# Moving a group norm to ScalarE and block sums to accumulating transfers in a two-attention convolution kernel

## The chip, the cores and the metric

The kernel runs on one core of a Trainium2 chip. Its engines work side by side: TensorE (PE, with its weight loads as PEld) multiplies, VectorE (DVE) and ScalarE (ACT) do elementwise work, GpSimd (POOL) a little of it, and SyncE (SP) only starts transfers. [...] The metric is the device time of one execution in microseconds (us).

## The reference

Sixteen images of 256 channels and 32 x 32 = 1024 positions pass through two blocks in float32. The source is cut to what is computed:

```python
def attention_block(x, w_proj, b_proj, w_out, b_out):     # 4 heads of 64
    xs = x.reshape(B, C, H * W).transpose(0, 2, 1)
    q, k, v = split(xs @ w_proj + b_proj)
    o = softmax(q @ k.T / sqrt(64)) @ v
    return (o @ w_out + b_out + xs).transpose(0, 2, 1).reshape(B, C, H, W)

def second_block(x):
    x = x + attention(group_norm(x, gn1_w, gn1_b))        # 8 heads of 32
    h = conv1x1(group_norm(x, gn2_w, gn2_b), mlp_w1, mlp_b1)   # 256 -> 1024
    return x + conv1x1(gelu(h), mlp_w2, mlp_b2)                # 1024 -> 256
```

A group norm takes 32 groups of 8 channels; its mean and variance run over 8 x 1024 values.

## The kernel before

**Tiling.** An image is held as 128 partitions x 2 channel halves x 1024 positions (`x`, three of them in rotation). Positions are cut into two halves t of 512 (`TB`), so that a product of 128 x 512 fills one bank of PSUM, the memory that TensorE writes. [...] three double tiles `s0`, `s1`, `s2` that `wide` hands out, the one longest unused first unless a number is given or a tile is kept back (`kept`), and two single banks `b0`, `b1` that `bank` hands out. A tile that is handed out again must first have been read by its last user.

**Stages of an image.** `attention_a` is the first attention: for 32 units it makes scores (`s_a`, L390), exponentials on ScalarE (`e_a`, L398), weighted values two units later (`acc_a`, L411) and sums of exponentials on VectorE (`es_a`, L423). When a half of the queries is done, the denominators are made (`den_a`, L442), copied by ScalarE, sent by a transfer to be spread over partitions, inverted on VectorE (L359), sent back through DRAM as `d_a`, and multiplied in (L468). The projection (`o`, L336) adds the result to `x` (L663) and takes the statistics of norm g (L666). In odd items of this attention the double tile `s2` holds the accumulator, and two double tiles are left for the scores.

Norm g of the image is worked out in the *gap* between the first attention and the keys and queries of the second (`qk_b`), and the gap is filled with *hidden pieces*: the first matrix of the MLP of the image before. `attention_b` is the second attention (`s_b` L524, `e_b` L539, `es_b` L555, `acc_b` L576, `den_b` L598), and its fill is the second matrix of the MLP of the image before (*output pieces*) and the first attention's keys, queries and values of the image after. The last projection of `attention_b` and norm h of the image are handed on into `attention_a` of the next image: norm h is applied there, among the exponentials, for images 0 to 14. While an attention runs, products are cut into narrow ones (`cols[0]` is 64 or 32 there); in the gap and for the last image's norm h, `cols[0]` is 128, which is `P`.

**The norm.** `group_norm` is a chain of steps with waits between: `averages` multiplies by a matrix that averages over groups (`gm`, `gv`), GpSimd takes the power -1/2 (L734), VectorE makes the scale and shift (`ga`, `gc`, L736 to L740), and L746 applies them: four VectorE operations of 128x512. For norm h five sums and differences of the result follow (`sums_of_input`, L875 to L879).

**The MLP** is made of two products in the manner of Strassen and Winograd, each with seven block products in place of eight. `begin`, `middle` and `finish` treat one of four row blocks each (i = 0 to 3), in the order begin 0, 1, middle 0, 1, finish 0, 1, and the same for 2, 3. Their products are L898, their evictions L911, L923 to L925 and L938, L939. Each `finish` ends with two subtractions (`combine` with minus, L954) between the four results of the Gelu. `reduce` makes a product of the second matrix; its order is 2, 5, 3, 4, 1, 6, 7. For products 2, 3, 4 the result is copied out of PSUM into `lent` by ScalarE and added to two blocks of `x` by VectorE (L1013), and then `combine` with plus adds four blocks for a later product (L954). When a block of `x` has all its sums, SP sends it out.

**Order.** The program's order is written out by hand: pieces are called in the order above, and `Later` calls a step after a number of ticks (a tick follows each unit and each piece). A scheduler then places instructions on their engines; `keep_in_program_order` pins one among its neighbours.

Of the kernel before, what the change touches and what calls it, by code (L numbers as in the profile page):

```python
# [8 lines left out]
F32 = mybir.dt.float32  # L9
I32 = mybir.dt.int32  # L10
AF = mybir.ActivationFunctionType
ALU = mybir.AluOpType
AX = mybir.AxisListType

P = 128
# [223 lines left out]
def first_pass(ctx, tc, x, out, k):  # L239
    nc = tc.nc  # L240
    B, C, S = x.shape
# [6 lines left out]
    small = ctx.enter_context(tc.tile_pool(name="small", bufs=2))  # L248
# [36 lines left out]
    def use(n):  # L285
        order.remove(n)
        order.append(n)

    def wide(name, n=None):
        if n is None:  # L290
            n = next(m for m in order if m not in kept)
        use(n)
        return ps_s.tile([P, 2, TB], F32, tag=f"s{n}", name=name)

    def bank(name, n):
        return ps_a.tile([P, TB], F32, tag=f"b{n}", name=name)
# [34 lines left out]
    cols = [P]  # L331
# [358 lines left out]
    def group_norm(key, src, stats, gw, gb, tag, out_tile, wait, then=None):  # L690
        st = {}

        def averages(name, src):
            if cols[0] == P:
                ps = bank(name, 1)
                product(ps[:, :CC], k["gavg"], src, start=True, stop=True)
                return [(slice(0, P), ps[:, :CC])]
            ps = wide(name)  # L700
            halves = [slice(h, h + HALF) for h in range(0, P, HALF)]
            for n, sl in enumerate(halves):
                nc.tensor.matmul(
                    ps[sl, n, :CC], k["gavg"][sl, sl], src[sl], start=True, stop=True
                )
            return [(sl, ps[sl, n, :CC]) for n, sl in enumerate(halves)]

        def means():
            mv = small.tile([P, CC, 2], F32, tag="mv", name=f"mv_{key}")
            for cc in range(CC):  # L710
                nc.vector.bn_aggr(mv[:, cc, :], stats[:, cc].rearrange("p t k -> p (t k)"))
            mean_c = small.tile([P, CC], F32, tag="mean_c", name=f"mean_c_{key}")
            nc.vector.tensor_copy(mean_c, mv[:, :, 0])
            st.update(mv=mv, mean_c=mean_c)
            later.after(wait, variances)

        def variances():
            mean = small.tile([P, CC], F32, tag="mean", name=f"mean_{key}")
            for sl, ps in averages(f"gm_{key}", st["mean_c"]):
                nc.vector.tensor_copy(mean[sl], ps)  # L720

            dv = small.tile([P, CC], F32, tag="dv", name=f"dv_{key}")
            nc.vector.tensor_sub(dv, st["mean_c"], mean)
            nc.vector.tensor_mul(dv, dv, dv)
            tv = small.tile([P, CC], F32, tag="tv", name=f"tv_{key}")
            nc.vector.tensor_add(tv, dv, st["mv"][:, :, 1])
            st.update(mean=mean, tv=tv)
            later.after(1 if cols[0] == P else 2, apply)

        def apply():  # L730
            rstd = small.tile([P, CC], F32, tag="rstd", name=f"rstd_{key}")
            for sl, ps in averages(f"gv_{key}", st["tv"]):
                nc.vector.tensor_scalar(rstd[sl], ps, EPS, None, ALU.add)
            nc.gpsimd.tensor_tensor(rstd, rstd, k["mhalf"], ALU.pow)  # L734
            a = small.tile([P, CC], F32, tag="ga", name=f"ga_{key}")
            nc.vector.tensor_mul(a, rstd, gw)  # L736
            ma = small.tile([P, CC], F32, tag="gma", name=f"gma_{key}")
            nc.vector.tensor_mul(ma, st["mean"], a)
            c = small.tile([P, CC], F32, tag="gc", name=f"gc_{key}")
            nc.vector.tensor_sub(c, gb, ma)  # L740
            y = act.tile([P, CC, S], F32, tag=tag, name=f"gn_{key}")
            out_tile.append(y)
            for t in range(NT):
                sl = slice(t * TB, (t + 1) * TB)
                for cc in range(CC):
                    nc.vector.tensor_scalar(  # L746
                        y[:, cc, sl], src[:, cc, sl],
                        a[:, cc : cc + 1], c[:, cc : cc + 1], ALU.mult, ALU.add,
                    )
            if then:  # L750
                then(y)

        means()
# [133 lines left out]
    def mlp(b, xb):  # L887
        n4 = HC // 2
        gs, open_sums = {}, {}
# [23 lines left out]
            )  # L913

        def begin(i):
            ps = wide(f"m1_{b}_{i}")
            if i % 2 == 0:
                open_sums["once"] = wide(f"m1_{b}_{i}_1")
            once = open_sums["once"][:, i % 2, :]
            open_sums[i] = ps  # L920
            products_of(i, [(2, ps[:, 0, :], True), (5, ps[:, 1, :], True), (1, once, True)])
            minus, rest = unit(0, 1, i), unit(1, 1, i)
            nc.scalar.activation(minus, ps[:, 0, :], AF.Copy, scale=-1.0)  # L923
            nc.vector.tensor_sub(rest, minus, ps[:, 1, :])  # L924
            nc.vector.tensor_add(rest, rest, once)  # L925
# [8 lines left out]
        def finish(i):  # L934
            ps = open_sums.pop(i)
            products_of(i, [(7, ps[:, 0, :], False), (6, ps[:, 1, :], False)])
            rest = gs[1, 1, i]
            nc.vector.tensor_add(unit(0, 0, i), rest, ps[:, 0, :])  # L938
            nc.vector.tensor_add(rest, rest, ps[:, 1, :])  # L939
            gelu(0, 0, i, gs[0, 0, i])  # L940
            gelu(1, 1, i, rest)
            combine((1, 0), (0, 0), False, i)
            combine((0, 1), (1, 1), False, i)

        hidden = [
            lambda part=part, i=i: part(i)
# [3 lines left out]

        def combine(to, what, plus, only=None):
            for i in range(n4) if only is None else (only,):
                d = gs[(*to, i)]
                (nc.vector.tensor_add if plus else nc.vector.tensor_sub)(  # L954
                    d, d, gs[(*what, i)]
                )

# [14 lines left out]
        def reduce(number, right, outs, then):  # L974
            ps = wide(f"m2_{b}_{number}")[:, 0, :]
            for i in range(n4):
                product(
                    ps, blocks[2][number - 1][:, i * P : (i + 1) * P], gs[(*right, i)],
                    start=(i == 0), stop=(i == n4 - 1),
                )  # L980
            bias, num = None, 1
            if len(outs) == 1:
                bias = k["m2b2"]

                num = 2 if b == B - 1 and number == 7 else 1
            elif number in (2, 5):
                bias = k["m2b"]
            co = outs[0][0]
            if len(outs) == 2:

                if not lent:
                    lent.append(act.tile([P, 4, TB], F32, tag="v0", name=f"lent_{b}"))
                m = lent[0][:, number % 4]
                if bias is not None:
                    nc.scalar.activation(m, ps, AF.Identity, bias=bias[:, co : co + 1])
                    bias = None
                else:
                    nc.scalar.copy(m, ps)
                ps = m

            def add_up():
                for co, t, plus in outs:
                    missing[co, t] -= 1
                    n = TB // num
                    for u in range(num):
                        sl = slice(t * TB + u * n, t * TB + (u + 1) * n)
                        y, p = xb[:, co, sl], ps[:, u * n : (u + 1) * n]
                        if bias is not None:
                            nc.vector.scalar_tensor_tensor(
                                y, p, bias[:, co : co + 1], y, ALU.add, ALU.add  # L1010
                            )
                        else:
                            (nc.vector.tensor_add if plus else nc.vector.tensor_sub)(y, y, p)  # L1013
                        if not missing[co, t]:
                            nc.sync.dma_start(out[b, co * P : (co + 1) * P, sl], y)
                if then:
                    combine(*then, True)


            if len(outs) == 2 and b < B - 1:  # L1020
                later.after(1, add_up)
            else:
                add_up()
# [32 lines left out]
    ps, n = bank("bqk", 0), brow.shape[0]  # L1056
# [32 lines left out]
    for b in range(B):  # L1089
# [3 lines left out]
        if b:  # L1093
# [4 lines left out]
                lambda st, b=b, xn=xn: group_norm(  # L1098
                    f"g{b}", xs[b], st, k["g1w"], k["g1b"], "res", xn, 2 if b else 3
                ),  # L1100
# [13 lines left out]
        n = len(qk) // CC  # L1114
# [352 lines left out]
```

## Time and profile before

| | us |
|---|---|
| median of 3 runs | 3700.3 (3698.66 to 3700.75) |
| profiled execution | 3700.6 |
| its span in the trace | 3698.8 |
| period of an image | 228.6 (one image of 230.3) |
| L746 norm h, 64 operations of 128x512 on VectorE | 30.6 |
| L746 norm g, 64 operations of 128x512 on VectorE | 30.6 |
| L1013, 160 operations on VectorE | 102.9 |
| GpSimd's transfers, all queues' bytes | 6.2 of 138.4 MB |

Busy times are sums over instructions of one engine within the span; engines work side by side, so they don't add up to the span. A group of instructions is written as line, engine, operation, output, inputs and shapes, with the count, the busy time and the mean of one. A timeline's row has the start and the time of a run of like instructions, and in square brackets how long the engine had been idle before it and what it waited for. The mean of one operation in a group is longer than the distance between two in a row, since neighbours overlap: the four operations of norm h take 1.92 us together at a mean of 543 ns.

### The profile page before, as it was taken

The numbers are of one execution on the slowest core, as the hardware profiler recorded it, in microseconds if no ns is written. First come the engines' busy times: TensorE is split into PE (matmuls) and PEld (weight loads), VectorE is DVE, ScalarE is ACT, GpSimd is POOL, SyncE is SP. The second block draws the span as 40 slices with busy tenths as digits, with TensorE's granted clock in tenths as the row PEclk, the third lists the DMA queues.
The fourth block names the chain that finished last, engine by engine and source line by source line (L and its number), as shares of the span: only waits on it lengthen the run. The fifth ranks groups of instructions, "written<-read, shape, count | busy, mean of one in ns | idle before, by whom it ended". The sixth has DMA issues, their size and how long they took to land.

```text
span 3698.8 us, 79399 instructions
## 1 busy us (share of the span) xinstructions
PE 3644.9 (99%) x34221; PEld 1290.8 (35%) x34221; DVE 2688.2 (73%) x3486; ACT 2118.4 (57%) x2768; POOL 121.1 (3%) x266
## 2 busy tenths in 40 slices
PE   9999999999999999999999999999999999999999
PEld 4333333333333333333333333333333333333333
DVE  4686767767677776777777777787777877677777
ACT  4665646556565665646656465564655656556572
POOL 3000000000000000000000000000000000000000
PEclk9999999999999999999999999999999999999999
DMA  4000110101101011010110101001010010101100
GB/s 146 11 16 30 53 33 13 50 30 53 33 14 50 30 53 33 19 49 28 50 33 19 50 27 50 32 19 50 27 56 27 23 46 33 50 27 42 36 28 27
DMA packets 66548, 138.35 MB, mean 37 GB/s; under 512 B 35630, under 2 KB 36398, under 8 KB 61966
## 3 DMA queue, kind: packets, MB, share of 16 engines
q1 hardware_dynamic: 63116, 126.64, 10.7%
q8 instruction: 270, 4.42, 0.5%
q0 software_dynamic: 1328, 6.17, 0.5%
q14 instruction: 88, 0.72, 0.1%
q10 hardware_dynamic: 1746, 0.40, 0.1%
HBM read 111.17 MB, written 21.23 MB: 36 GB/s over the span
## 4 chain that ended last, share of the span: by engine, by line
PE 81%; DVE 14%; issue 3%; DMA 1%; ACT 1%; POOL 1%; SPq 0%; DVEq 0%; ACTq 0%
PE s_b L524 12%; PE acc_b L576 12%; PE m L336 10%; PE s_a L390 9%; PE acc_a L411 8%; PE m L898 6%; PE qk_a L336 6%; PE qk_b L336 5%; DVE es_a L423 4%; PE v_a L336 3%; PE j L336 3%; PE v_b L336 2%; PE den_b L598 1%; DVE g L954 1%; DVE es_b L555 1%
## 5 line engine op out<-in xcount | busy, mean ns | idle before, releaser
L539 ACT ACTIVATE e_b<-s_b 128x1024 f32<-128x1024 f32 (+1 forms) x1280 | 983.0, 864 | 151.0 <-PE s_b L524 151.0
L555 DVE TENSOR_TENSOR es_b<-es_b,e_b 128x1024 f32<-128x1024 f32 x768 | 899.1, 1218 | 217.3 <-ACT e_b L539 217.2
L398 ACT ACTIVATE e_a<-s_a 128x1024 f32<-128x1024 f32 x512 | 521.3, 1025 | 360.1 <-PE s_a L390 345.7
L524 PE MATMUL s_b<-q,k 32*64 32x512 f32 x8192 | 526.9, 601 | 9.8 <-DVE v L793 7.0
L390 PE MATMUL s_a<-q,k 64*64 64x512 f32 x4096 | 532.6, 593 | 1.1
L411 PE MATMUL acc_a<-e_a,v 64*64 64x512 f32 x4096 | 528.5, 589 | 0.0
L423 DVE TENSOR_TENSOR es_a<-es_a,e_a 128x1024 f32<-128x1024 f32 x384 | 471.0, 1226 | 58.4 <-ACT e_a L398 39.1
L576 PE MATMUL acc_b<-e_b,v 128*32 128x512 f32 x4096 | 493.8, 600 | 0.0
L336 PE MATMUL m<-g,w 128*32 128x512 f32 (+1 forms) x3320 | 404.3, 592 | 0.0
L524 PEld LDWEIGHTS s_b<-q,k 32*64 32x64 f32 x8192 | 166.1, 130 | 337.3 <-issue 127.7
L411 PEld LDWEIGHTS acc_a<-e_a,v 64*64 64x64 f32 x4096 | 161.9, 133 | 277.5 <-issue 236.1
L390 PEld LDWEIGHTS s_a<-q,k 64*64 64x64 f32 x4096 | 152.6, 133 | 278.1 <-issue 208.2
L898 PE MATMUL m<-gn_h,w 128*128 128x512 f32 x512 | 243.7, 604 | 5.7 <-DVE g L924 3.3
L589 DVE TENSOR_TENSOR res_b<-res_b,acc_b 128x512 f32<-128x512 f32 x192 | 131.6, 686 | 145.5 <-PE acc_b L576 145.5
L336 PE MATMUL qk_b<-gn_g,wq 128*32 128x512 f32 (+1 forms) x1280 | 235.7, 594 | 1.7
L576 PEld LDWEIGHTS acc_b<-e_b,v 128*32 128x32 f32 x4096 | 108.6, 109 | 358.2 <-ACT e_b L539 194.8
L336 PE MATMUL qk_a<-x,wp 128*32 128x512 f32 (+1 forms) x1856 | 233.5, 592 | 0.0
L336 PEld LDWEIGHTS m<-g,w 128*32 128x32 f32 (+1 forms) x3320 | 121.4, 112 | 262.3 <-issue 235.0
L954 DVE TENSOR_TENSOR g<-g,g 128x512 f32<-128x512 f32 x320 | 206.0, 680 | 4.0 <-ACT g L911 2.8
L898 PE MATMUL m<-hs,w 128*128 128x512 f32 x384 | 177.9, 592 | 0.1
L555 DVE TENSOR_TENSOR es_b<-e_b,e_b 128x1024 f32<-128x1024 f32 x128 | 150.6, 1217 | 0.0
L911 ACT ACTIVATE g<-g,m1b 128x512 f32<-128x512 f32 x128 | 92.1, 722 | 99.6 <-DVE g L938 72.7
(146 smaller groups left out, 2793.5 us busy)
## 6 DMA issues: line engine op xcount, KB each, us to landing
w<-w_kept SPq DMA_DIRECT2D x30, 1792.0 KB
d_a<-row_a SPq DMA_DIRECT2D x64, 256.0 KB
rd_b<-row_b SPq DMA_DIRECT2D x252, 64.0 KB
out_dram<-x SPq DMA_DIRECT2D x63, 256.0 KB
x<-in_x_dram SPq DMA_DIRECT2D x30, 512.0 KB
w_kept<-w_made POOLq DMA_DIRECT2D x2, 1792.0 KB, 7.1
w_made<-in_L_conv_mlp_w_dram POOLq DMA_DIRECT2D x8, 256.0 KB, 6.5
x<-in_x_dram SPq DMA_DIRECT2D x4, 256.0 KB
```

Source lines behind the costliest of these rows:

```text
L336: nc.tensor.matmul(o[sl], w[:, sl], r, **flags)
L390: nc.tensor.matmul(s[h : h + HALF, g, :], kT[g * D : (g + 1) * D, c, kb * P + h : kb * P + h + HALF], qT[g * D : (g + 1) * D, c, t * TB : ...
L398: nc.scalar.activation(e, s, AF.Exp, scale=float(D) ** -0.5)
L411: nc.tensor.matmul(accs[i][h][g * D : (g + 1) * D, :], v[h * HALF : (h + 1) * HALF, kb, c * 2 + g], e[h * HALF : (h + 1) * HALF, g, :], st ...
L423: nc.vector.tensor_add(sums[i], held[i] if kb == 1 else sums[i], e)
L524: nc.tensor.matmul(outs[g][h : h + HALF, :], kT[g * D : (g + 1) * D, c, k0 : k0 + HALF], qT[g * D : (g + 1) * D, c, t * TB : (t + 1) * TB] ...
L539: nc.scalar.activation(to, s, AF.Exp, scale=float(D) ** -0.5)
L555: ins = nc.vector.tensor_add(d, es[n % 2] if kb == 0 else d, es[n])
L576: nc.tensor.matmul(acc[g * D : (g + 1) * D, :], v[:, kb + m, c * G + g], es[2 * m + g // 2][:, g % 2, :], start=(m == 0), stop=(m == 1),)
L589: nc.vector.tensor_add(r, r, acc)
L898: nc.tensor.matmul(ps, blocks[1][number - 1][:, i * P : (i + 1) * P], inputs[b][number], start=first, stop=True, skip_group_check=not first,)
L954: (nc.vector.tensor_add if plus else nc.vector.tensor_sub)(d, d, gs[(*what, i)])
```

## The change

- *Norm h on ScalarE.* Where `cols[0]` isn't `P` (norm h of images 0 to 14) the four operations of a norm become ScalarE activations with the scale and shift as per-partition operands. Norm g and the last norm h stay on VectorE.
- *The averages in the gap* go into the double tile `s2` and no longer into the bank `b1`.
- *The hidden pieces' PSUM.* `begin(i)` takes the double tile i % 2 and the bank i % 2; before, it took double tiles in turn, and two row blocks shared one more of them.
- *An early Gelu* of 128x1 in `begin(0)`.
- *The subtractions* of the four row blocks come after `finish(3)`, all eight of them, pinned in order; for the last image they stay where they were.
- *Sums by transfers.* For images 0 to 14 the additions of `combine` with plus and of `reduce` for products with two outputs, where they are plain sums, become transfers that GpSimd starts and that add to what stands at their destination. Subtractions and the additions with a bias stay on VectorE.

```diff
@@ group_norm, averages
             if cols[0] == P:
-                ps = bank(name, 1)
+                ps = wide(name, 2)[:, 0, :]
@@ group_norm, apply
-                    nc.vector.tensor_scalar(
-                        y[:, cc, sl], src[:, cc, sl],
-                        a[:, cc : cc + 1], c[:, cc : cc + 1], ALU.mult, ALU.add,
-                    )
+                    if cols[0] == P:
+                        nc.vector.tensor_scalar(
+                            y[:, cc, sl], src[:, cc, sl],
+                            a[:, cc : cc + 1], c[:, cc : cc + 1], ALU.mult, ALU.add,
+                        )
+                    else:
+                        nc.scalar.activation(
+                            y[:, cc, sl], src[:, cc, sl], AF.Identity,
+                            bias=c[:, cc : cc + 1], scale=a[:, cc : cc + 1],
+                        )
@@ mlp, begin
-            ps = wide(f"m1_{b}_{i}")
-            if i % 2 == 0:
-                open_sums["once"] = wide(f"m1_{b}_{i}_1")
-            once = open_sums["once"][:, i % 2, :]
+            if i == 0:
+                few = small.tile([P, 1], F32, tag="few", name=f"few_{b}")
+                tc.keep_in_program_order(
+                    nc.scalar.activation(few, k["mhalf"][:, :1], AF.Gelu)
+                )
+            ps, once = wide(f"m1_{b}_{i}", i % 2), bank(f"m1_{b}_{i}_1", i % 2)
@@ mlp, finish
-            combine((1, 0), (0, 0), False, i)
-            combine((0, 1), (1, 1), False, i)
+            for n in (i,) if b == B - 1 else range(n4) if i == n4 - 1 else ():
+                combine((1, 0), (0, 0), False, n)
+                combine((0, 1), (1, 1), False, n)
@@ mlp, combine
-                d = gs[(*to, i)]
-                (nc.vector.tensor_add if plus else nc.vector.tensor_sub)(
-                    d, d, gs[(*what, i)]
-                )
+                d, g = gs[(*to, i)], gs[(*what, i)]
+                if plus and b < B - 1:
+                    nc.gpsimd.dma_start(d, g, accum_op=ALU.add)
+                    continue
+                ins = (nc.vector.tensor_add if plus else nc.vector.tensor_sub)(d, d, g)
+                if not plus:
+                    tc.keep_in_program_order(ins)
@@ mlp, reduce, add_up
+                        elif plus and b < B - 1:
+                            nc.gpsimd.dma_start(y, p, accum_op=ALU.add)
                         else:
                             (nc.vector.tensor_add if plus else nc.vector.tensor_sub)(y, y, p)
```

## The prediction

> **What bounds the kernel now.** I read the page's busy times first, then TensorE's waits, then windows over one image, then the timeline of the stretches that the change touches.
>
> ```profile
> PE 3644.9 (99%) x34221; PEld 1290.8 (35%) x34221; DVE 2688.2 (73%) x3486; ACT 2118.4 (57%) x2768; POOL 121.1 (3%) x266
> ```
>
> TensorE is the bound, at a granted clock of 1.00: 3698.8 - 3644.9 = 53.9 us of the span is all that work elsewhere can win. What does TensorE wait for?
>
> ```profile
> PE den_a L442 <- DVE res_a L428: 28.1, 15, 1.9
> PE s_b L524 <- DVE v L793: 7.0, 16, 1.2
> PE m L898 <- DVE g L924: 3.3, 15, 1.0
> ```
>
> Total, times, longest. One wait stands out: 28.1 / 15 = 1.87 us per image, and VectorE ends it. Windows over a typical image (start 674.9, period 228.6 us) are two parts of the first attention, the gap (hidden pieces and norm g), the queries and keys, and the second attention; the columns are wall time, then busy time of PE, PEld, DVE, ACT and POOL.
>
> ```profile
> 674.90:710.40 35.50, 35.50 (x340) 12.37 (x344) 21.50 (x21) 21.37 (x23) 1.69 (x4) 1.00 0.21 69
> 710.40:738.80 28.40, 26.50 (x248) 9.41 (x248) 26.08 (x42) 14.38 (x15) 0.70 (x1) 1.00 0.07 20
> 738.80:770.30 31.50, 31.19 (x101) 13.39 (x101) 21.51 (x44) 12.98 (x20) 1.14 (x3) 1.00 0.06 18
> 770.30:805.00 34.70, 34.37 (x364) 13.53 (x368) 21.36 (x24) 23.21 (x32) 0.00 (x0) 1.00 0.15 54
> 805.00:903.30 98.30, 98.30 (x1140) 30.62 (x1132) 77.02 (x89) 60.49 (x84) 2.00 (x6) 1.00 0.09 28
> ```
>
> Only the second row loses much (1.90 us), and there VectorE is full (26.08 of 28.40). In the second attention TensorE loses nothing, although VectorE is busy for 77.02 us.
>
> [...] The trace's nearest rows are lower: a Gelu of that shape from SBUF with one pointer, 722 ns, and an Identity from PSUM, 688 ns. The trace decides. [...] the trace has copies between exponentials without a load. [...] The eight 256 KB loads on that queue landed in 3.5 to 10.4 us here, median 7.1[...].
>
> **Part A: ScalarE normalises norm h, in the first attention.**
>
> ```profile
> 718.45 1.02 ACT L398 ACTIVATE e_a<-s_a 128x1024 f32<-128x1024 f32 x1 [0.69 <-PE s_a L390]
> 720.28 1.02 ACT L398 ACTIVATE e_a<-s_a 128x1024 f32<-128x1024 f32 x1 [0.81 <-PE s_a L390]
> 722.30 0.16 DVE L740 TENSOR_TENSOR gc_h<-g2b,gma_h 128x2 f32<-128x2 f32 x1
> 722.49 1.92 DVE L746 TENSOR_SCALAR gn_h<-x,ga_h,gc_h 128x512 f32<-128x512 f32 x4
> 722.91 1.04 PE L390 MATMUL s_a<-q,k 64*64 64x512 f32 x8
> ...
> 735.04 1.92 PE L336 MATMUL o<-res_a,wo 128*32 128x512 f32 x16
> 738.10 0.68 DVE L428 TENSOR_TENSOR res_a<-res_a,acc_a 128x512 f32<-128x512 f32 x1
> 738.83 1.07 PE L442 MATMUL den_a<-es_a,ones 128*32 128x256 f32 x16 [1.87 <-DVE res_a L428]
> ```
>
> Images 0 to 14 move four operations each (60 in all). In the changed program's order on ScalarE they stand between the exponentials that begin here at 718.45 and 720.28. They wait for gc_h (ends 722.46), so ScalarE blocks from 719.47, and behind the block is queued the exponential of 720.28, whose PSUM tile TensorE needs two score tiles later: in this stretch only two of the three double banks rotate.
>
> Price: 0.72 us each, overlapped by 0.1 as the trace's pairs of Gelu are (two of 0.684 take 1.27), gives a pitch of 0.62. The four take 722.5 + 4 x 0.62 = 724.98; the delayed exponential ends at 726.01; TensorE's scores begin at 726.08 and not at 722.91. New stall: 3.17 us; 2.95 at a pitch of 0.56[...]. I take 3.17, since the rows are of this shape.
>
> What this releases: the old wait of 1.87 (2.08 between the end of matmuls of modelled pitch and their start) was for VectorE's chain, which runs back to back from its 1.92 us of gn_h to L428. On ScalarE the last gn_h ends at about 725.1, VectorE's input sums keep pace a pitch behind, and its chain ends only about 0.1 us later than before, or up to 0.9 if the last copy (L427) comes late. TensorE comes to den_a at 735.04 + 3.17 + 1.72 + 0.09 = 740.02, later than either: the old stall is covered by the new one. Net: 740.02 - 738.83 = +1.19 us per image, bounds +0.97 and +1.6. A stall of 3 us at the start replaces one of 2 us at the end.
>
> **Part B: the gap.** Times from den_a's start D.
>
> ```profile
> 751.94 1.22 DVE L468 TENSOR_TENSOR res_a<-res_a,d_a 128x1024 f32<-128x1024 f32 x1 [3.68 <-DMA d_a<-row_a]
> 754.53 3.60 PE L336 MATMUL o<-res_a,wo 128*128 128x512 f32 x8
> 761.72 1.12 PE L898 MATMUL m<-gn_h,w 128*128 128x512 f32 x2 [0.16 <-DVE g L924]
> 770.27 1.98 PE L336 MATMUL qk_b<-gn_g,wq 128*128 128x512 f32 x4
> ```
>
> Before, the projection o starts at D + 15.70 and the queries at D + 31.44. Four of the eight subtractions (L954, 0.68 us each: 2.7 us) stand ahead of norm g on VectorE; the change puts all eight after the last finish, beside attention's keys, where VectorE is busy for 21.36 of 34.70 us. Single banks replace the shared double tiles, and one product more of the hidden pieces moves behind o (14 matmuls of 0.857 us stand ahead of it, not 15). So o can start at D + 15.07; then 18 matmuls of 0.857 us and some 0.5 us of short waits give the queries at D + 31.0. Gain 0.45 to 0.6; its ceiling is what is lost there now, 0.35 (L924) + 0.30 (release by L939) + 0.28 (gm, gv) = 0.93. I take -0.5, bounds -0.2 and -0.9. The early table load (128x1 Gelu) lies in ScalarE's idle 4.21 us ahead of d_a's copy: nothing; the trace's load takes 1.28 us, so without that cover it would cost up to that.
>
> **Part C: accumulating transfers.** For images 0 to 14, 12 sums of products' inputs and 8 of outputs, all 128x512, leave VectorE:
>
> ```profile
> L954 DVE TENSOR_TENSOR g<-g,g 128x512 f32<-128x512 f32 x320 | 206.0, 680 | 4.0 <-ACT g L911 2.8
> ```
>
> 20 x 0.68 = 13.6 us of VectorE per image, all in the stretch where TensorE is 98.30 of 98.30 busy: gain 0. In their place stand 20 transfers per image, 300 in all, 78.6 MB. Each costs GpSimd an issue (544 to 792 ns in the eight loads' rows, so about 15 us per image on an engine with 2.00 us of work there). Four stand together every 7 us or so, and their results are used 20 us or more later; at 7.1 us to landing, hidden. Other queues: SP's output transfers of two blocks now wait for a landing, and behind the first of them stands the spread of the denominators; in an image I followed it moves from about 613.3 to 615.5 us, and its reciprocal is wanted on VectorE at 622.6: slack some 5 us. GpSimd's running sums of denominators stand behind issues, with no user near. The bound on the gain is 0; on the cost, 0 if a transfer lands within about 10 us, 1 to 3 us per image if they serialise and the slack goes. I take 0.
>
> **The last image** keeps VectorE's sums, but its rstd_h on GpSimd (3640.25 before) stands behind x_14's transfers, issued by about 3637.5: -1 to +3 us, once; I take 0.
>
> **Sum.** 15 x (1.19 - 0.5) = +10.3 us. The profiled execution took 3700.6 us (span 3698.8 and 1.8 around it), the median of the runs is 3700.3: 3710 on either.
>
> **The rivals.**
> 1. *The stall of part A doesn't come, and the old one goes* (faster). If the scores at 722.91 can run without the delayed exponential, or its delay stays under the tile's slack, VectorE's relief of 1.92 us decides: 15 x (-1.9 - 0.5) = -36, 3664 us. For it: VectorE carries the stretch. Against it: that exponential ends at 721.30 and those scores start at 722.91, a slack of 1.6 us, and the block delays it by 4.7 us (724.99 - 720.28). The rival decides from the point where the delay is under 1.6 us, so if gc_h came about 3 us earlier than 722.46, which nothing in the diff brings about; halfway there it would give about 3690.
> 2. *Even*: A at +0.97, B at -0.9: 15 x 0.07, about 3701.
> 3. *The transfers are slow* (slower by more). At over about 2 us each in series, an output transfer blocks SP, then the reciprocal, the exponentials' eight buffers and TensorE: 1 to 3 us per image on top, 3725 to 3755. For it: GpSimd's issue beside a VectorE that is 78% busy isn't shown by the trace. Against it: DMA share is 0.09 there.
> 4. *VectorE's 13.6 us reach TensorE*: nothing to reach, 98.30 of 98.30. It adds nothing.
>
> **How the numbers follow.** The forecast, part A by 0.97 to 1.6 and B by -0.2 to -0.9, spans 3701 to 3721: chance 0.50. Rival 1 and its halves 0.13, rival 2 0.17, rival 3 0.20. A measurement of this kernel tells 0.2%, 7.4 us, from no change. Faster by that: rival 1, 0.13. Within it: rival 2 and the forecast's lower end, 0.28. Slower: 0.59. The range leaves a tenth at each end: 3692, into rival 1's half, to 3730, into rival 3.
>
> **What would show it.** Right: gn_h on ACT at about 0.72 us with its wait on gc_h; TensorE's scores waiting about 3 us for e_a fifteen times; den_a's wait on L428 gone; qk_b at about D + 31.0; VectorE down by 300 x 0.68 + 60 x 0.5 = 234 us; the GpSimd queue up by 78.6 MB; the second attention's stretch unchanged. Wrong: no such wait of s_a (rival 1), or TensorE losing time between 805 and 903 (rival 3).

## The result and the profile after

The changed kernel takes 3729.6 us (median of 4 runs, 3729.1 to 3731.0) against 3700.3: a ratio of 1.0081, 95% interval 1.0063 to 1.0098. It is slower by 29 us where 10 were forecast. The busy times and two transfer queues of the page after:

```profile
PE 3657.1 (98%) x34221; PEld 1293.1 (35%) x34221; DVE 2506.1 (67%) x3126; ACT 2159.1 (58%) x2844; POOL 383.0 (10%) x566
q0 software_dynamic: 44528, 84.84, 12.9%
q1 hardware_dynamic: 63116, 126.64, 10.6%
```

The change does what it says: VectorE is busy for 182 us less (the 360 operations that left it took 235 us one by one, but busy time counts overlapping neighbours once), ScalarE gains 41, GpSimd's queue carries 78.7 MB more. But TensorE, with the same 34221 instructions, is busy for 12 us longer. TensorE's waits after (total, times, longest):

```profile
PE s_a L390 <- ACT e_a L398: 49.4, 15, 3.3
PE s_b L524 <- DVE v L800: 7.0, 16, 1.2
PE o L336 <- DVE res_a L468: 3.0, 15, 0.3
```

The wait of den_a is gone and one of 3.29 us per image for ScalarE's exponential stands in its place. The cause in ScalarE's groups, and one image in its timeline:

```profile
L753 ACT ACTIVATE gn_h<-x,gc_h,ga_h 128x512 f32<-128x512 f32 x60 | 43.9, 802 | 45.2 <-DVE gc_h L740 45.2
```

```profile
1187.57 2.93 ACT L753 ACTIVATE gn_h<-x,gc_h,ga_h 128x512 f32<-128x512 f32 x4 [3.01 <-DVE gc_h L740]
1190.40 1.91 ACT L398 ACTIVATE e_a<-s_a 128x1024 f32<-128x1024 f32 x2
```

ScalarE works these off in the program's order: it waits 3.01 us for gc_h, then works for 2.93 on the four normalisations (802 ns each, one every 0.71), and only then makes the exponential that TensorE needs, although its scores had been ready since 1185.31. Windows of another image by stage, with the columns of those in the prediction:

```profile
910.20:945.70 35.50, 35.50 (x344) 12.37 (x340) 21.58 (x21) 21.37 (x23) 1.67 (x4) 1.00 0.21 68
945.70:975.60 29.90, 26.55 (x252) 9.50 (x252) 24.43 (x37) 16.96 (x19) 0.71 (x1) 1.00 0.07 19
975.60:1007.00 31.40, 31.20 (x105) 13.56 (x98) 19.95 (x39) 13.25 (x21) 1.14 (x3) 1.00 0.07 18
1007.00:1041.60 34.60, 34.27 (x364) 13.26 (x367) 23.88 (x28) 23.00 (x32) 0.00 (x0) 1.00 0.15 54
1041.60:1139.90 98.30, 98.30 (x1136) 30.62 (x1128) 65.38 (x69) 60.47 (x84) 18.93 (x26) 1.00 0.41 82
```

This image has a period of 229.7 us. The second attention is unchanged at 98.30 of 98.30, although VectorE does 11.6 us less there and GpSimd 16.9 us more; the stretch with the stall is 1.5 us longer. But only 6 of the 14 periods from image 1 on are of 229.7; 7 are of 231.4, and the first is of 232.6. TensorE's timeline behind the stall, first in an image of the short kind, then in one of the long kind:

```profile
957.40 1.04 PE L411 MATMUL acc_a<-e_a,v 64*64 64x512 f32 x8
961.73 1.09 PE L390 MATMUL s_a<-q,k 64*64 64x512 f32 x8 [3.29 <-ACT e_a L398]
962.64 1.04 PE L411 MATMUL acc_a<-e_a,v 64*64 64x512 f32 x8
963.50 1.04 PE L390 MATMUL s_a<-q,k 64*64 64x512 f32 x8
```

```profile
1187.12 1.04 PE L411 MATMUL acc_a<-e_a,v 64*64 64x512 f32 x8
1191.46 1.62 PE L390 MATMUL s_a<-q,k 64*64 64x512 f32 x8 [3.30 <-ACT e_a L398]
1192.83 1.95 PE L411 MATMUL acc_a<-e_a,v 64*64 64x512 f32 x8
1194.54 1.42 PE L390 MATMUL s_a<-q,k 64*64 64x512 f32 x8
1195.78 1.04 PE L411 MATMUL acc_a<-e_a,v 64*64 64x512 f32 x8
```

The stalls are alike, but in the second image the matmuls behind it take up to 1.95 us in place of 1.04. The granted clock (the third number from the end) explains it. Each pair of windows is 3.41 us in which the stall ends, and the 3.41 us behind it:

```profile
959.78:963.20 3.42, 1.47 (x16) 0.65 (x20) 3.09 (x5) 3.42 (x6) 0.00 (x0) 1.00 0.00 0
963.20:966.61 3.41, 3.41 (x40) 1.20 (x36) 3.38 (x5) 2.03 (x3) 0.00 (x0) 1.00 0.02 5
1188.48:1191.89 3.41, 0.43 (x4) 0.21 (x8) 2.05 (x4) 3.41 (x5) 0.00 (x0) 1.00 0.01 2
1191.89:1195.31 3.42, 3.42 (x20) 1.07 (x16) 3.39 (x5) 1.91 (x3) 0.00 (x0) 0.50 0.02 5
```

In the long images TensorE runs at a clock of 0.50 for 3.41 us just behind the stall (a *dip* from here on), which costs 1.70 us. Nine of the 15 stalls have one; in the first of them it lasts for 6.83 us and costs 2.84. So the span's growth adds up, with D the start of den_a in an image:

| part, in the profiled executions | us |
|---|---|
| from the start of an image's first attention to D: 65.47 for 64.02, 15 x 1.45 | +21.8 |
| clock behind the stall: 8 x 1.70, and 2.84 in the first | +16.4 |
| from D to the next first attention, images 1 to 14: 164.26 for 164.57, 14 x -0.31 | -4.3 |
| one image before had late denominators (period 230.26) | -1.7 |
| up to the first attention of image 1 +0.4, behind the last D -2.2 | -1.8 |
| sum; the spans are 3729.14 and 3698.76 | +30.4 |

### The profile page after: what moved, and what is told of

Its sections match the earlier page's. It is cut to its first block, busy times and chain, and to the rows that moved or that the text cites. A ratio compares the mean times of both kernels' runs of the same rounds, so it can differ in the third digit from the quotient of the medians.

```text
span 3729.1 us, 79988 instructions
## 1 busy us (share of the span) xinstructions
PE 3657.1 (98%) x34221; PEld 1293.1 (35%) x34221; DVE 2506.1 (67%) x3126; ACT 2159.1 (58%) x2844; POOL 383.0 (10%) x566
## 4 chain that ended last, share of the span: by engine, by line
PE 92%; DVE 3%; issue 2%; ACT 2%; DMA 1%; SPq 0%; POOL 0%; DVEq 0%; ACTq 0%
PE s_b L524 13%; PE acc_b L576 12%; PE s_a L390 12%; PE acc_a L411 11%; PE m L336 10%; PE m L905 10%; PE qk_a L336 6%; PE qk_b L336 5%; PE o L336 3%; PE v_a L336 3%; PE j L336 3%; PE v_b L336 2%; PE den_b L598 1%; ACT gn_h L753 1%; PE den_a L442 1%
## 5 line engine op out<-in xcount | busy, mean ns | idle before, releaser
L390 PE MATMUL s_a<-q,k 64*64 64x512 f32 x4096 | 542.3, 602 | 50.2 <-ACT e_a L398 49.4
L411 PE MATMUL acc_a<-e_a,v 64*64 64x512 f32 x4096 | 536.9, 598 | 0.0
L968 POOL DMA_DIRECT2D g<-g x180 | 162.8, 1099 | 742.7 <-DVE es_b L555 673.4
L1029 POOL DMA_DIRECT2D x<-lent x120 | 140.4, 1500 | 258.5 <-ACT lent L1014 137.3
```

The costliest lines, as they stand in the source:

```text
L390: nc.tensor.matmul(s[h : h + HALF, g, :], kT[g * D : (g + 1) * D, c, kb * P + h : kb * P + h + HALF], qT[g * D : (g + 1) * D, c, t * TB : ...
L411: nc.tensor.matmul(accs[i][h][g * D : (g + 1) * D, :], v[h * HALF : (h + 1) * HALF, kb, c * 2 + g], e[h * HALF : (h + 1) * HALF, g, :], st ...
L968: nc.gpsimd.dma_start(d, g, accum_op=ALU.add)
L1029: nc.gpsimd.dma_start(y, p, accum_op=ALU.add)
```

## The experiments

The theory: the whole loss is ScalarE's block, as a stall and as the clock that the stall costs; the transfers are hidden; the gap gains. The rivals: the transfers or the gap's new order cost something, or the clock has another cause. A first set undoes or isolates one part each.

**Norm h back on VectorE**, all else as changed:

```diff
-                    if cols[0] == P:
+                    if True:
                         nc.vector.tensor_scalar(
```

> The changed kernel with norm h back on VectorE; all other parts of the change stay. Theory (the whole loss is ScalarE's block in the first attention: a stall of TensorE of 3.3 us per image, and after it, in 9 of 15 images, matmuls at about half clock for some 3.4 us, 1.7 us each): no stall of s_a, no clock dip behind it, the old wait of 1.87 us at den_a back, the gap's gain of 0.3 us per image kept: 3690 to 3697 us. Rival (the accumulating transfers or the gap's new order cost something): over 3705 us.

Measured: 3693.0 us, ratio 0.9982 (0.9975 to 0.9989). All 14 periods are of 228.3 us, and no image has a dip (mean granted clock 0.999, for 0.995 in the changed kernel). The wait of the kernel before is back:

```profile
PE den_a L442 <- DVE res_a L428: 28.3, 15, 1.9
PE o L336 <- DVE res_a L468: 3.0, 15, 0.2
```

What is left of the change is a small gain.

**Norm h on ScalarE alone**, in the kernel before:

```diff
-                    nc.vector.tensor_scalar(
-                        y[:, cc, sl], src[:, cc, sl],
-                        a[:, cc : cc + 1], c[:, cc : cc + 1], ALU.mult, ALU.add,
-                    )
+                    if cols[0] == P:
+                        nc.vector.tensor_scalar(
...
+                    else:
+                        nc.scalar.activation(
+                            y[:, cc, sl], src[:, cc, sl], AF.Identity,
+                            bias=c[:, cc : cc + 1], scale=a[:, cc : cc + 1],
+                        )
```

> The kernel before with norm h on ScalarE and no other part of the change. Theory: 15 x 1.45 us of net stall plus dips of 1.7 us in 8 to 12 images, without the gap's gain: 3733 to 3743 us, granted clock about 0.995. Rival (the other parts cause a share of the loss): under 3725 us.

Measured: 3740.3 us, ratio 1.0110 (1.0094 to 1.0125), with 10 dips in 15 images (mean granted clock 0.995): the loss is whole without any other part of the change.

**The sums back on VectorE**:

```diff
-                if plus and b < B - 1:
+                if False:
                     nc.gpsimd.dma_start(d, g, accum_op=ALU.add)
...
-                        elif plus and b < B - 1:
+                        elif False:
                             nc.gpsimd.dma_start(y, p, accum_op=ALU.add)
```

> The changed kernel with the 300 sums back on VectorE and no accumulating transfer. Theory: TensorE didn't notice them, so 3729.6 us give or take two dips of 1.7 us: 3726 to 3733. Rival (transfers in the way of others, GpSimd late): 3719 or less.

Measured: 3731.3 us, ratio 1.0085 (1.0071 to 1.0098), at a mean granted clock of 0.995, as with the transfers.

**The stall filled.** Twelve matmuls whose result nobody reads stand in front of the waiting scores:

```diff
+WARM = 12
...
+            if b and i == 3 and kb == 2:
+                warm = ps_s.tile([P, 2, TB], F32, tag="s2", name=f"warm_{b}")
+                for _ in range(WARM):
+                    nc.tensor.matmul(
+                        warm[:, 0, :P], k["gavg"], k["gavg"], start=True, stop=True
+                    )
             s = wide(f"s_{key}_{i}_{kb}")
```

> The changed kernel with twelve 128x128 matmuls without use (about 2.6 us) placed in TensorE's stall, ahead of the scores that wait for ScalarE. The wait itself stays. Theory (an idle TensorE loses its clock): the scores start no later than before, no clock dip behind them, 1.45 us per image net stays: 3711 to 3716 us, granted clock 0.999. Rival (the dips have another cause, or cost nothing): 3728 to 3732 us with the dips in place.

Measured: 3715.7 us, ratio 1.0043 (1.0029 to 1.0057). The timeline of one image, whose line numbers are 9 higher for the scores here:

```profile
1183.62 1.04 PE L420 MATMUL acc_a<-e_a,v 64*64 64x512 f32 x8
1184.59 2.94 PE L393 MATMUL warm<-gavg 128*128 128x128 f32 x24
1187.95 1.09 PE L399 MATMUL s_a<-q,k 64*64 64x512 f32 x8 [0.42 <-ACT e_a L407]
1188.86 1.04 PE L420 MATMUL acc_a<-e_a,v 64*64 64x512 f32 x8
```

The trace has two records for each of these matmuls. The scores still start 4.33 us after the last weighted values (1187.95 - 1183.62, and 4.34 in the changed kernel), so ScalarE's block is untouched. Yet no dip follows any of the 15 stalls: all 14 periods are of 229.73, and the mean granted clock is 0.999. (A drop of the clock in this trace is at 144.3 us, in image 0, which has no such stall.) Work without use made the kernel 14 us faster, which the rival can't explain: the clock that was lost behind these stalls comes from TensorE's idleness in them.

A second set asks for sizes, and for what is left. **Two operations on ScalarE, two on VectorE**, still ahead of the exponential:

```diff
-                    if cols[0] == P:
+                    if cols[0] == P or t == 1:
```

> The changed kernel with the first two of norm h's four operations on ScalarE, still ahead of the same exponential, and the other two on VectorE. Theory (each operation on ScalarE delays the exponential by 0.70 us): stall 3.29 - 2 x 0.70 = 1.9 us, TensorE reaches den_a about when it does in the kernel before, VectorE's chain is 1 us shorter so its wait is gone; no clock dip, as none followed the waits of 1.87 us: 3691 to 3696 us, no better than norm h on VectorE altogether. Rival (VectorE's relief is worth something by itself): below 3686.

Measured: 3693.3 us, ratio 0.9983 (0.9976 to 0.9990); a stall of 1.89 us in 15 images, no dip (mean granted clock 0.999). **Three on ScalarE**:

```diff
-                    if cols[0] == P:
+                    if cols[0] == P or (t, cc) == (1, 1):
```

> The changed kernel with three of the four operations on ScalarE ahead of the exponential and one on VectorE. Theory: stall 2.6 us, net +0.75 us per image over norm h on VectorE: 3704 us without clock dips. Open is how long TensorE may idle: if 2.6 us still trips the clock in half the images, 3717[...].

Measured: 3708.6 us, ratio 1.0026 (1.0016 to 1.0037). That is neither of the two answers but between them: stalls of 2.59 us, and a dip of 1.70 us of cost in 4 of 15 images (mean granted clock 0.998). One more operation thus costs 0.70 us of stall per image each time: 1.89, 2.59, 3.29.

**The gap's parts alone** (both undoings above together: norm h and the sums on VectorE):

> The kernel before with the gap's parts of the change alone: single banks, postponed subtractions, early Gelu; norm h and the sums stay on VectorE. Theory (the transfers are hidden): as with norm h back on VectorE and the transfers kept, 3693 us: 3690 to 3696. Rival (the transfers cost or gain): more than 3 us away from 3693.

Measured: 3693.4 us, ratio 0.9984 (0.9977 to 0.9990). With the transfers it was 3693.0: they neither cost nor gain. Which of the gap's parts gives the small gain that is left was not separated.

**Two operations behind the exponential.** The same work, in another place: two on VectorE at once, two on ScalarE one and two score tiles later, pinned:

```diff
...
+            for n, (cc, t) in enumerate(((0, 0), (1, 1), (1, 0), (0, 1))):
+                if cols[0] == P or n < 2:
+                    normalise(cc, t, False)
+                else:
+                    later.after(n - 1, lambda cc=cc, t=t: normalise(cc, t, True))
...
```

> The changed kernel with two operations of norm h on VectorE, and two on ScalarE placed behind the exponential that TensorE waits for, one before and one after the next exponential. Theory (place decides, not the engine): no stall of s_a, VectorE's chain 0.96 us shorter, so den_a's wait falls from 1.9 to about 0.9 us: 3693 - 15 x 0.96 = 3679 us, 3676 to 3684. Rival (any normalisation among the exponentials stalls TensorE): 3690 or more.

Measured: 3680.8 us, ratio 0.9953 (0.9938 to 0.9967), 19 us faster than the kernel before. The waits:

```profile
PE den_a L442 <- DVE res_a L428: 15.3, 15, 1.3
PE s_b L524 <- DVE v L806: 7.1, 16, 1.2
```

No wait of s_a is left, and den_a waits 1.0 us per image for 1.9. Against 3693.3 us with two operations ahead of the exponential, the place alone is worth 12 us. (The new order of the four blocks holds for norm g too, but the stretch from D to the next first attention takes 164.28 us, as in the kernel with norm h on VectorE.) **Three behind the exponential**, with `n < 1` and `later.after(n, ...)`:

> As the kernel with two operations on ScalarE behind the exponential, with three there (one ahead of each of the next exponentials, one at a time) and one on VectorE. Theory: another 0.48 us per image off VectorE's chain, if VectorE isn't left waiting for the normalised blocks: 3681 - 15 x 0.48 = 3674 us at best; it now waits for exponentials at the end of its chain, so half of that is likelier: 3674 to 3681. Rival (VectorE waits for ScalarE in place of the work that it was spared, or TensorE waits for the later exponentials): 3681 or more.

Measured: 3682.8 us, ratio 0.9955 (0.9942 to 0.9969): no better, so the expectation missed and its rival stands. den_a waits 16.0 us in all, no less than with two (15.3). From the end of gc_h to its last addition ahead of den_a VectorE takes 15.59 us per image (15.55 with two on ScalarE): its operations there add up to 0.53 us less, but it waits for 0.45 us more, 0.30 of it until ScalarE has normalised a block that VectorE sums up:

```profile
DVE hs L888 <- ACT gn_h L752: 4.5, 15, 0.3
```

## Why the prediction was wrong

- *The step that failed: TensorE's clock stands nowhere in the sum.* The prediction read "a granted clock of 1.00", and its sum, 15 x (1.19 - 0.5), gives the forecast stall of 3.17 us no other cost than its length. The clock that followed the stalls cost 16.4 us in the profiled execution, more than the whole forecast of 10.3. The trace of the kernel before could have warned of it, since it has such a drop itself: in the last image, 0.50 from 3543.27 to 3546.68, behind an idle time of 1.22 us. Half clock over these 3.41 us loses 1.7 us, an estimate from that row; the changed kernel's images with a dip are 1.70 us longer. How many of the 15 stalls would bring a dip, that trace doesn't show.
- *Part A's mechanism was right, its price too low.* The stall came 15 times, where it was said, and took the place of den_a's wait; TensorE, not VectorE, then decided when den_a starts. The step that was mis-sized is "The trace decides": I took 0.72 us and a pitch of 0.62 from Gelus with one pointer. The trace after has 802 ns, and each operation adds 0.70 us of stall. The measured row of a like shape (722 ns), with one operand fewer, was not the same operation. The scores came 3.45 us late where 3.17 stood, so the net is +1.45 and not +1.19 per image: 3.9 us in all, within the bound of 1.6.
- *Part B* was right in kind. The queries start at D + 31.18, not 31.0; the wait for L468 before o (3.0 us over 15 images) takes part of it. The stretch from D to the next first attention is 0.31 us shorter in the changed kernel and 0.29 with norm h on VectorE, where 0.5 was taken and 0.2 was the lower bound: -4.3 us where -7.5 stood, 3.2 us of the error.
- *Part C* was right: zero, by both pairs of runs (3693.0 with and 3693.4 without the transfers; 3729.6 and 3731.3, apart by what one dip costs). An issue took 1.10 us of GpSimd on average for one kind of sum and 1.50 for the other, about twice what the eight loads had shown, and stayed hidden.
- *The last image* ends 2.2 us sooner (214.6 for 216.8 us after D). The drop of the clock at 3543.27 in the kernel before accounts for 1.7 of it: the kernel with norm h on ScalarE alone, whose last image is as before but has no such drop, ends 1.7 us sooner (215.1). The gap gives 0.3.
- *The rivals.* Rival 1 named what would win, an exponential delayed by less than its slack of 1.6 us, and rightly said that nothing in the diff brings it about; the kernel with two operations behind the exponential does, for half of VectorE's relief. Rival 3 didn't occur: its range of 3725 to 3755 holds the measured time by luck, and so does the outer range of 3692 to 3730, since no sum there contained the clock.

From 10.3 the sum runs: + 3.9 (price) + 3.2 (gap) + 16.4 (clock) - 1.7 - 1.8 = 30.3, against spans that differ by 30.4.

## What to carry to other kernels

Moving work from a full engine to an idle one helped here only where it stood behind the instructions that the bounding engine waits for: while ScalarE waited 3.01 us for a late operand, an exponential whose scores were ready waited behind it. A forecast stall of TensorE is to be priced with the clock that follows it: 1.89 us cost only its length here, 2.59 and 3.29 us cost 1.70 us more in 4 and in 9 of 15 images (2.84 in one of the nine). A stall that can't be removed can be filled with matmuls of no use, which gave 14 us here. The price of an operation is best taken from a row with the same operands: here a Gelu of the same shape with one pointer fewer gave 722 ns where the operation took 802.

## What the runs showed of the hardware

Stalls of 1.89 us (two operations on ScalarE, 15 images) lost no clock, 2.59 us (three) did in 4 of 15, 3.29 us in 9 of 15 (changed kernel) and 10 of 15 (norm h on ScalarE alone). The stalls of the changed kernel are of 3.29 or 3.30 us, so their length doesn't pick the images. Its trace shows what goes with the dips. In this trace and in that of the kernel before, all changes of the granted clock lie on one grid of 3.413 us, to 0.01 us. The nine stalls with a dip left TensorE idle for 2.23 to 3.05 us between two edges of this grid, and the clock fell at the second of them; the six without a dip left it idle for 1.65 to 2.01 us in the step with more of it. In the two pairs of windows above, which lie on this grid, it was idle for 1.95 us (3.42 - 1.47) without a dip, and for 2.98 us (3.41 - 0.43) with one. So the stall that ends at 500.57 us, which an edge cuts into 1.70 and 1.59, lost no clock.

The first stall's dip lasted for 6.83 us, two steps of the grid. It is the only one of the nine with idle time behind the edge at which the clock fell: 2.23 us ahead of it and 1.05 us behind it.

Idle time doesn't tell all of it. The drop at 3543.27 in the kernel before, and that at 144.3 in the kernel with the stall filled, follow only 1.22 us of idle time, in the second attention. In the kernel before:

```profile
3539.85:3543.27 3.42, 2.21 (x28) 0.50 (x20) 3.34 (x4) 2.92 (x5) 0.00 (x0) 1.00 0.00 0
3543.27:3546.68 3.41, 3.41 (x20) 0.86 (x19) 0.00 (x0) 1.02 (x1) 0.00 (x0) 0.50 0.00 0
```

Windows with more idle time, up to the 2.01 us above, kept the clock. What tells them apart is open.
